# Weights loaded piece by piece between the tiles, and the levels of all tiles on VectorE, in the opening loop of a quantised cross-attention

## The chip, the cores and the metric

The kernel runs on one core of a Trainium2 chip. Five engines work side by side, each through its own list of instructions in order: PE (TensorE, matrix products; its weight loads are listed as PEld), DVE (VectorE), ACT (ScalarE), POOL (GpSimd) and SP (SyncE, which here issues the transfers between the chip's memory and the on-chip buffers). They wait for one another by semaphores. The metric is the time of one execution in microseconds on the device, lower is better.

## What is computed

Four transformer blocks follow one another over x of 4 x 1024 rows of 288, with a context of 64 rows for each of the 4. Blocks 0 and 3 have 8-bit linear layers, block 1 is a pair of cross-attentions. The change lies in block 2, whose second attention goes to the context and is fake-quantised:

```python
def _fake_quant(x, n_bits, always_zero=False):
    levels = float(2 ** n_bits - 1)
    if always_zero:
        delta = jnp.max(x) / levels
        zp = 0.0
    else:
        xmin, xmax = jnp.min(x), jnp.max(x)
        delta = (xmax - xmin) / levels
        zp = jnp.round(-xmin / delta)
    xq = jnp.clip(round(x / delta) + zp, 0.0, levels)
    return (xq - zp) * delta

def _quant_attention(x, ctx, Wq, Wk, Wv, Wo, bo):
    q, k, v = heads(x @ Wq), heads(ctx @ Wk), heads(ctx @ Wv)
    q, k, v = _fake_quant(q, 8), _fake_quant(k, 8), _fake_quant(v, 8)
    probs = softmax(q @ k.T / sqrt(18))
    probs = _fake_quant(probs, 8, always_zero=True)
    return merge(probs @ v) @ Wo + bo

h = h + _quant_attention(_ln(h), ctx, Wq2, Wk2, Wv2, Wo2, bo2)
proj = _ln(h) @ Wff1 + bff1
a, gate = jnp.split(proj, 2, axis=-1)
h = h + a * gelu(gate) @ Wff2 + bff2
```

There are 16 heads of 18. The step of the probabilities, `delta`, needs the largest probability over all rows before a single one can be rounded, so the scores are computed twice: once for their largest values and sums, once for the result.

## The kernel before

The 4096 rows are 32 tiles of 128 (`NT` = 32, 8 for each of the 4 parts of the batch). Block 2 is `fq_attn`, and its context attention and feed-forward part are `fq_tail` (L3481). Its raw queries wait in memory as `rawq`; `fq_tail` begins by loading them into `qn`, four transfers of 1152 KB, with the operands made of the keys (`kbd4`, `kbd`, `vbd`) between them.

Then comes the loop that the change touches (from L3609 on). It goes over groups `n` of four tiles. For each tile, `largest(t, qT)` (L3539) does this:

- it turns the raw queries into levels, in place: multiply by the reciprocal step and add a large constant (L819), subtract it again and take the maximum with the lower bound (L820), both in `fq_levels`; then it clips to the upper bound into one of three buffers `pads`, in bf16 (L3545). Tiles 0 to 2 and the even ones do it on DVE, the odd ones from tile 3 on POOL;
- PE transposes the four groups of heads (L3551), and ACT copies them to the group's `qT` (L3554), a buffer of which there are two, so that group `n` writes where group `n - 2` was;
- SP writes the tile's part of `qT` to memory, `qb` (L3555), for the second pass;
- PE multiplies with `kbd4` (L3558), and DVE takes the largest score of each head (L3565, `top`).

`total(n, qT)` (L3569) is a generator that runs one step after each following tile: four products (L3576) with an exponential each on ACT (L3581), their sums over the keys through products with `pick` (L3587), a copy by ACT to `sT` (L3592), products with `back` (L3596), then on DVE the sums, their reciprocals, the largest probability and its maximum (L3604 to L3607).

After the first group, the loop also loads what the feed-forward part needs: two vectors of the layer norm, the weights `w1` by `load_halves` (L2650), `w2` by `load_w` (L115), and the biases. `load_halves` loads the first 256 of the 288 rows in one transfer (L2654). The last 32 rows, which stand four times over in the array, are kept as a rounded half and a remainder: for each of six pieces of 384 columns a transfer into a scratch tile `y` with two buffers (L2660), a cast on DVE (L2661), and on the lower 64 partitions a subtraction (L2662), into the tile `w1h`. The pieces are done in one go, one behind the other. `load_halves` also serves the first attention of this block (L3031), with two pieces of 432 columns.

The order of instructions on PE, DVE, ACT and POOL is set by a scheduler from the dependences and the order of the program. On SP the order is the program's own here (`tc.manual_schedule` around `fq_tail`): an issue that waits holds up all that stand behind it.

Of the kernel before, what the change touches and what calls it, by code (L numbers as in the profile page):

```python
# [28 lines left out]
F32 = mybir.dt.float32  # L29
# [4 lines left out]
ALU = mybir.AluOpType  # L34
# [3 lines left out]
P = 128  # L38
B, S, C, H, D, T, FF = 4, 1024, 288, 16, 18, 64, 1152
# [1141 lines left out]
class Fast(Net):  # L1181
# [1465 lines left out]
            )  # L2647


    def load_halves(self, pool, scratch, w, n, name, step):  # L2650

        nc = self.nc
        t = pool.tile([P, 2, n], F32, name=name)
        nc.sync.dma_start(t, w[: 2 * P].rearrange("(c p) o -> p c o", p=P))  # L2654
        c = pool.tile([P, n], F32R, name=f"{name}h")
        for c0 in range(0, n, step):
            m = min(step, n - c0)
            cols = slice(c0, c0 + m)
            y = scratch.tile([P, step], F32, tag="w3", name="w3", bufs=2)[:, :m]
            nc.sync.dma_start(y, w[2 * P :, cols])  # L2660
            nc.vector.tensor_copy(c[:, cols], y)  # L2661
            nc.vector.tensor_tensor(  # L2662
                c[64:, cols], y[64:], c[64:, cols].bitcast(F32), ALU.subtract
            )
        return t, c

    def halves_T(self, dst, dstc, src):

# [812 lines left out]
    def fq_tail(self, w, kq, keep, rawq, mx, nmn, beside):  # L3481
# [4 lines left out]
        tc, nc = self.tc, self.nc  # L3486
        with ExitStack() as es:
            pool = lambda name, bufs, **k: es.enter_context(tc.tile_pool(name=name, bufs=bufs, **k))
# [5 lines left out]
            wp = pool("f3w", 1)  # L3494
# [7 lines left out]
            with (  # L3502
# [7 lines left out]
                qn = qp.tile([P, NT, C], F32, name="qn")  # L3510
# [8 lines left out]
                q = self.global_params(gp, mx, nmn, "qq")  # L3519
                self.watch_range(-0.5, 255.5, q["zp"], "qzext")  # L3520
                step = gp.tile([P, 1], F32, name="step")
# [17 lines left out]
                def largest(t, qT):  # L3539

                    b, j = divmod(t, NTB)
                    pd = pads[t % 3]
                    eng = nc.gpsimd if t > 2 and t % 2 else nc.vector
                    self.fq_levels(qn[:, t, :], q, 0, eng)
                    eng.tensor_scalar(  # L3545
                        pd[:, :, :D], self.heads(qn[:, t, :]), q["top"], None, ALU.min
                    )
                    ps = self.ps1(BF16)
                    pf = pd.rearrange("p h d -> p (h d)")
                    for g in range(NG):  # L3550
                        nc.tensor.transpose(  # L3551
                            ps[:, g * P : (g + 1) * P], pf[:, g * P : (g + 1) * P], self.idb
                        )
                    nc.scalar.copy(qT, ps[:, : NG * P].rearrange("p (g t) -> p g t", t=P))  # L3554
                    nc.sync.dma_start(qb[b][:, :, j * P : (j + 1) * P], qT)  # L3555
                    ps = self.ps2()
                    for g in range(NG):
                        nc.tensor.matmul(  # L3558
                            ps[:, g // 2, g % 2 * 256 : (g % 2 + 1) * 256],
                            lhsT=qT[:, g, :],  # L3560
                            rhs=kt["kbd4"][:, b, g, :],
                            start=True,
                            stop=True,
                        )
                    nc.vector.tensor_reduce(  # L3565
                        top[:, t, :], ps.rearrange("p a (h k) -> p (a h) k", k=T), AX.X, ALU.max
                    )

                def total(n, qT):  # L3569

                    es_ = []
                    for g in range(NG):
                        ps = self.ps2()
                        for pr in range(2):
                            rows = slice(pr * 64, (pr + 1) * 64)
                            nc.tensor.matmul(  # L3576
                                ps[:, pr, :], lhsT=kt["kbd"][rows, n // 2, g, :],
                                rhs=qT[rows, g, :], start=True, stop=True,
                            )
                        e = self.wk.tile([P, 2, 512], F32, tag="e1", name="e1", bufs=6)  # L3580
                        nc.scalar.activation(e, ps, AF.Exp, scale=rstep)  # L3581
                        es_.append(e)
                        yield
                    acc = self.ps1()
                    for pr in range(2):
                        for g in range(NG):
                            nc.tensor.matmul(  # L3587
                                acc[g * HP : (g + 1) * HP, :], lhsT=pick[:, pr, :],
                                rhs=es_[g][:, pr, :], start=(pr == 0), stop=(pr == 1),
                            )  # L3590
                    sT = self.wk.tile([P, 512], F32, tag="sT", name="sT", bufs=1)
                    nc.scalar.copy(sT, acc)  # L3592
                    yield
                    ps = self.ps1()
                    for j in range(4):
                        nc.tensor.matmul(  # L3596
                            ps[:, j * H : (j + 1) * H], lhsT=sT[:, j * P : (j + 1) * P],
                            rhs=back, start=True, stop=True,
                        )
                    part = lambda a: a[:, 4 * n : 4 * n + 4, :].rearrange("p t h -> p (t h)")  # L3600
                    self.ended = nc.scalar.activation(
                        part(most), part(top), AF.Exp, scale=rstep
                    ).ins
                    nc.vector.tensor_copy(part(sums), ps[:, : 4 * H])  # L3604
                    nc.vector.reciprocal(part(rs), part(sums))
                    nc.vector.tensor_tensor(part(most), part(most), part(rs), ALU.mult)
                    nc.vector.tensor_reduce(tmx[:, n : n + 1], part(most), AX.X, ALU.max)  # L3607

                running = []  # L3609
                for n in range(NT // 4):  # L3610
                    qT = self.wk.tile([P, NG, 512], BF16, tag="qT1", name="qT1", bufs=2)
                    for j in range(4):
                        largest(4 * n + j, qT[:, :, j * P : (j + 1) * P])
                        if n == 0 and j == 3:
                            nc.sync.dma_start(qT0, qb[0][:, :, : 4 * P])
                        running = [t for t in running if next(t, running) is not running]
                    running.append(total(n, qT))
                    if n == 0:
                        g3 = self.load_bc(wp, w["ln3_g"], C, "g3")
                        b3 = self.load_bc(wp, w["ln3_b"], C, "b3")  # L3620
                        nf = FF // P
                        w1 = self.load_halves(wp, qp, w["Wff13"], 2 * FF, "w1", 384)
                        w2 = self.load_w(wp, w["Wff2"], C, "w2", p=P)
                        bf1 = wp.tile([P, 2 * nf], F32, name="bf1")
                        nc.sync.dma_start(bf1, w["bff1"])
                        bf2 = self.load_bc(wp, w["bff2"], C, "bf2")
                while running:
                    running = [t for t in running if next(t, running) is not running]
                flat = lambda ap: ap.rearrange("p t h -> p (t h)")
# [170 lines left out]
            for t0 in range(0, NT, 4):  # L3800
# [14 lines left out]
                for j in range(4):  # L3815
                    next(after, None)
                    cols = slice(j * P, (j + 1) * P)
# [188 lines left out]
```

## Time and profile before

| | us |
|---|---|
| three runs: lowest, median, highest | 4733.14, 4738.31, 4739.08 |
| the profiled execution | 4733.92 |
| its span, first to last instruction | 4732.1 |
| queries loaded, first level on DVE | 2858.25 |
| first product with `kbd4` | 2865.36 |
| cast of the first piece of w1 | 2899.49 |
| copy of tile 12 by ACT | 2913.61 |
| maximum of tile 12 by DVE | 2915.33 |
| last write of `qb` issued | 2965.32 |
| end of the sums, last maximum of a probability | 2981.34 |
| products of the feed-forward part with `w1h` | 3033.7 to 3533.4 |

The profile's times of single instructions count from the start of the span. A line of the order of time reads: start, time taken, engine, line of the program, operation, tiles written and read, their shapes, how many instructions were merged into the line, and in brackets how long the engine had been idle before and what ended the idling. A line of the waits reads: who waited for whom, the sum in us, how often, and the longest. The mean TensorE clock that was granted over the whole span was 0.88 of full speed.

### The profile page before, as it was taken

The numbers are of one execution on the slowest core, as the hardware profiler recorded it, in microseconds if no ns is written. First come the engines' busy times: TensorE is split into PE (matmuls) and PEld (weight loads), VectorE is DVE, ScalarE is ACT, GpSimd is POOL, SyncE is SP. The second block draws the span as 40 slices with busy tenths as digits, with TensorE's granted clock in tenths as the row PEclk, the third lists the DMA queues.
The fourth block names the chain that finished last, engine by engine and source line by source line (L and its number), as shares of the span: only waits on it lengthen the run. The fifth ranks groups of instructions, "written<-read, shape, count | busy, mean of one in ns | idle before, by whom it ended". The sixth has DMA issues, their size and how long they took to land. (4 is left out here: it accounts for less than half of the span.)

```text
span 4732.1 us, 62855 instructions
## 1 busy us (share of the span) xinstructions
PE 4196.1 (89%) x22841; PEld 1741.1 (37%) x22841; DVE 3077.9 (65%) x6914; ACT 2999.1 (63%) x4277; POOL 1193.8 (25%) x1797
## 2 busy tenths in 40 slices
PE   4999998889988889999789986899998999998887
PEld 2223323455566531111123333455552233223444
DVE  8355445786644779999888986544346446446886
ACT  2776776566753259999799973322215776775665
POOL 2001001333210567440013343210101000002453
PEclk9999999889999875555589997899998999998898
DMA  3000002110000321000001014001001000001000
GB/s 88 2 6 22 9 11 54 56 42 6 13 13 17 113 92 42 27 18 0 14 21 29 26 29 144 21 21 19 0 19 26 2 10 26 7 12 39 15 18 19
DMA packets 138592, 135.92 MB, mean 29 GB/s; under 512 B 69404, under 2 KB 116124, under 8 KB 136736
## 3 DMA queue, kind: packets, MB, share of 16 engines
q1 hardware_dynamic: 137072, 128.13, 9.2%
q0 software_dynamic: 1200, 3.69, 0.4%
q8 instruction: 181, 2.97, 0.3%
q14 instruction: 139, 1.14, 0.1%
HBM read 79.92 MB, written 43.47 MB: 26 GB/s over the span
## 5 line engine op out<-in xcount | busy, mean ns | idle before, releaser
L2196 ACT ACTIVATE e<-ps 128x1024 f32<-128x1024 f32 x1024 | 992.6, 1021 | 412.0 <-PE ps L2186 404.6
L2186 PE MATMUL ps<-qT,kT 32*128 32x512 f32 x4096 | 624.3, 647 | 2.0 <-DVE sext L2108 2.0
L3251 DVE TENSOR_REDUCE top<-e 128x2 f32<-128x2048 f32 x256 | 563.5, 2273 | 15.4 <-ACT e L3244 15.2
L2142 PE MATMUL ps<-e,v 128*32 128x512 f32 x4096 | 553.9, 612 | 9.0 <-DVE oT L2153 9.0
L3842 PE MATMUL ps<-qk 32*128 32x512 bf16 x1024 | 500.7, 604 | 40.3 <-ACT e L3244 38.6
L3244 ACT ACTIVATE e<-ps 128x1024 f32<-128x1024 f32 x512 | 521.6, 1190 | 6.6 <-PE ps L3842 3.1
L3891 ACT ACTIVATE e<-ps 128x1024 f32<-128x1024 f32 x512 | 477.1, 1080 | 33.3 <-PE ps L3882 18.5
L3897 DVE TENSOR_SCALAR eb<-e 128x2048 bf16<-128x2048 f32 x256 | 323.8, 1270 | 48.4 <-ACT e L3891 47.3
L1921 POOL TENSOR_TENSOR x<-x,y 128x288 f32<-128x288 f32 x188 | 149.1, 805 | 812.2 <-DVE y L1919 484.8
L2693 PE MATMUL psf<-hT,w 128*128 128x512 f32 x576 | 271.9, 594 | 0.7 <-ACT hT L2684 0.6
L2186 PEld LDWEIGHTS ps<-qT,kT 32*128 32x128 f32 x4096 | 184.8, 185 | 202.1 <-issue 130.3
L3882 PE MATMUL ps<-qk,kz 64*128 64x512 bf16 x1024 | 216.7, 423 | 32.3 <-ACT e L3891 27.4
L2142 PEld LDWEIGHTS ps<-e,v 128*32 128x32 f32 x4096 | 81.3, 108 | 402.7 <-issue 345.0
L3842 PEld LDWEIGHTS <-qk 32*128 32x128 bf16 x1024 | 53.1, 99 | 465.6 <-issue 464.6
L3758 ACT ACTIVATE gl<-psf,bf 128x512 f32<-128x512 f32 x72 | 49.3, 685 | 243.6 <-PE psf L2694 235.0
L2038 POOL TENSOR_TENSOR v<-y,wv1b 128x288 f32<-128x288 f32 x64 | 51.0, 802 | 565.1 <-DVE y L2035 565.1
L3244 ACT ACTIVATION_READ_ACCUMULATOR e<-ps 128x1 f32 x512 | 192.1, 375 | 0.0
L1535 POOL TENSOR_TENSOR h<-h,g 128x288 f32<-128x288 f32 x108 | 88.0, 815 | 355.5 <-ACT h L1532 355.5
L279 PEld LDWEIGHTS <-qT 98*128 98x128 bf16 (+2 forms) x1344 | 130.1, 103 | 127.4 <-ACT qT L1437 38.9
L2153 DVE COPY oT<-ps 128x512 f32<-128x512 f32 x64 | 44.1, 689 | 202.0 <-PE ps L2142 202.0
L3762 DVE SCALAR_TENSOR_TENSOR u<-psf,bf,gl 128x512 f32<-128x512 f32 x72 | 53.6, 748 | 153.0 <-PE psf L2694 152.8
L3773 PE MATMUL psf<-w,u 128*128 128x288 f32 x576 | 147.0, 410 | 0.0
(579 smaller groups left out, 7970.4 us busy)
## 6 DMA issues: line engine op xcount, KB each, us to landing
raw<-y SPq DMA_DIRECT2D x32, 432.0 KB
in<-raw SPq DMA_DIRECT2D x30, 432.0 KB
kz<-qk SPq DMA_DIRECT2D x128, 64.0 KB
wn<-in_L_wfc SPq DMA_DIRECT2D x12, 432.0 KB
x<-in_x SPq DMA_DIRECT2D x4, 1152.0 KB
vvo<-vt SPq DMA_DIRECT2D x16, 288.0 KB
vo<-vvo SPq DMA_DIRECT2D x4, 1152.0 KB
qn<-rawq SPq DMA_DIRECT2D x4, 1152.0 KB
```

The costliest lines, as they stand in the source:

```text
L1921: eng.tensor_tensor(self.x[:, t, :], self.x[:, t, :], y, ALU.add)
L2142: nc.tensor.matmul(acc[i * HP : (i + 1) * HP, :], lhsT=st["v"][:, kt, h * (D + 1) : h * (D + 1) + HP], rhs=es_[i // 2][:, i % 2, :], start ...
L2186: nc.tensor.matmul(pss[i // 2][:, i % 2, :], lhsT=self.row_tile(kT, i)[:, kt * P : (kt + 1) * P], rhs=self.row_tile(qT, i)[:, qh * 512 : ( ...
L2196: nc.scalar.activation(e, ps, AF.Exp, scale=SCALE)
L2693: nc.tensor.matmul(o, lhsT=a[:, c, :], rhs=b[:, c, :], start=(c == 0), stop=False)
L3244: nc.scalar.activation(e[:, j, :].rearrange("p (a n) -> p a n", a=2), sc, AF.Exp, scale=rstep, accum_out=sums[:, t, h0 + j : h0 + j + 1],)
L3251: nc.vector.tensor_reduce(top[:, t, h0 : h0 + 2], e, AX.X, ALU.max)
L3773: nc.tensor.matmul(ps[:, :C], lhsT=us[f][:, j * P : (j + 1) * P], rhs=w2[:, f, :], start=(f == 0), stop=(f == nf - 1),)
L3842: self.last = self.nc.tensor.matmul(ps[:, c, :], lhsT=self.row_tile(qT, i)[:, g, qt * P : (qt + 1) * P], rhs=self.row_tile(kT, i)[:, g, c ...
L3882: nc.tensor.matmul(pss[i][:, n, :], lhsT=kz[rows, i, kt * P : (kt + 1) * P], rhs=qT[rows, g, qh * 512 : (qh + 1) * 512], start=True, stop= ...
L3891: nc.scalar.activation(e[:, 2 * n : 2 * n + 2, :], ps, AF.Exp, scale=step)
L3897: nc.vector.tensor_scalar(eb, e, MAGIC, MAGIC, ALU.add, ALU.subtract)
```

## The change

Two things are changed. `load_halves` is split: `halves_pieces` loads the first 256 rows and returns a generator that does one piece at each step. `load_halves` now runs that generator to its end and is the same as before. The loop in `fq_tail` takes the generator instead, and goes one step after each tile from tile 4 on; what is left would be done behind the loop. So the six pieces come after tiles 4 to 9, in the order of the program, and `w2` and the biases come ahead of them. Second, `largest` gives all three operations of the levels to DVE for every tile.

```diff
-    def load_halves(self, pool, scratch, w, n, name, step):
+    def halves_pieces(self, pool, scratch, w, n, name, step):
 
         nc = self.nc
         t = pool.tile([P, 2, n], F32, name=name)
         nc.sync.dma_start(t, w[: 2 * P].rearrange("(c p) o -> p c o", p=P))
         c = pool.tile([P, n], F32R, name=f"{name}h")
-        for c0 in range(0, n, step):
...
-        return t, c
+
+        def pieces():
+            for c0 in range(0, n, step):
+                m = min(step, n - c0)
+                cols = slice(c0, c0 + m)
+                y = scratch.tile([P, step], F32, tag="w3", name="w3", bufs=2)[:, :m]
+                nc.sync.dma_start(y, w[2 * P :, cols])
+                nc.vector.tensor_copy(c[:, cols], y)
+                nc.vector.tensor_tensor(
+                    c[64:, cols], y[64:], c[64:, cols].bitcast(F32), ALU.subtract
+                )
+                yield
+
+        return (t, c), pieces()
+
+    def load_halves(self, *a):
+
+        t, pieces = self.halves_pieces(*a)
+        for _ in pieces:
+            pass
+        return t
...
-                    eng = nc.gpsimd if t > 2 and t % 2 else nc.vector
-                    self.fq_levels(qn[:, t, :], q, 0, eng)
-                    eng.tensor_scalar(
+                    self.fq_levels(qn[:, t, :], q, 0)
+                    nc.vector.tensor_scalar(
                         pd[:, :, :D], self.heads(qn[:, t, :]), q["top"], None, ALU.min
                     )
...
-                running = []
+                running, pieces = [], iter(())
                 for n in range(NT // 4):
...
                         running = [t for t in running if next(t, running) is not running]
+                        next(pieces, None)
                     running.append(total(n, qT))
                     if n == 0:
...
-                        w1 = self.load_halves(wp, qp, w["Wff13"], 2 * FF, "w1", 384)
+                        w1, pieces = self.halves_pieces(wp, qp, w["Wff13"], 2 * FF, "w1", 384)
                         w2 = self.load_w(wp, w["Wff2"], C, "w2", p=P)
...
+                for _ in pieces:
+                    pass
                 while running:
```

More of the change, by code (lines that the diff above doesn't have):

```diff
@@ L2655, in load_halves @@
         c = pool.tile([P, n], F32R, name=f"{name}h")
-        for c0 in range(0, n, step):
[L2657 to L2664, printed above, removed]
-        return t, c
+        def pieces():
[15 more added lines that the diff above has]
+        return t
     def halves_T(self, dst, dstc, src):
```

## The prediction

> **What bounds the kernel now.** I read the page first, for the engines' shares, then the stage that the diff touches: its stretches, the waits of ACT and SP in it, and its instructions in order of time.
>
> ```profile
> span 4732.1 us, 62855 instructions
> PE 4196.1 (89%) x22841; PEld 1741.1 (37%) x22841; DVE 3077.9 (65%) x6914; ACT 2999.1 (63%) x4277; POOL 1193.8 (25%) x1797
> ```
>
> PE carries the kernel as a whole. The change lies in the opening loop of `fq_tail`, from 2858 to about 2981 us, where the shares differ:
>
> ```profile
> core 0: us, PE busy (x) PEld busy (x) DVE busy (x) ACT busy (x) POOL busy (x), PEclk, DMA share, GB/s
> 2876.00:2899.00 23.00, 17.11 (x92) 6.62 (x90) 18.10 (x33) 9.53 (x14) 19.22 (x21) 0.78 0.37 144
> 2899.00:2914.00 15.00, 0.09 (x2) 0.00 (x0) 5.77 (x13) 0.39 (x1) 0.00 (x0) 0.64 0.71 199
> 2930.00:2950.00 20.00, 18.14 (x120) 7.59 (x119) 12.56 (x20) 12.25 (x20) 4.00 (x4) 1.00 0.21 53
> ```
>
> In the second row 15 us pass in which PE does nothing. The waits of ACT (first line) and of SP's queue in this stage, and the instructions, tell why:
>
> ```profile
> ACT qT L3554 <- DMA qb<-qT: 15.0, 1, 15.0
> SPq L2660 <- DVE w1h L2662: 16.5, 4, 14.7
> ```
> ```profile
> 2898.07 0.58 ACT L3592 COPY sT<-ps 128x512 f32<-128x512 f32 x1 [2.10 <-PE ps L3587]
> 2899.20 0.37 DVE L3545 TENSOR_SCALAR pads<-qn,qqtop 128x288 bf16<-128x288 f32 x1 [3.79 <-PE ps L3551]
> 2899.49 0.35 DVE L2661 CAST w1h<-w 128x384 fp32r<-128x384 f32 x1
> 2905.29 0.42 SPq L115 DMA_DIRECT2D w<-in_L_Wff  x1
> 2906.45 8.97 SPq L3555 DMA_DIRECT2D qb<-qT  x10
> 2913.61 1.07 ACT L3554 COPY qT<-ps 128x512 bf16<-128x512 bf16 x2 [14.96 <-DMA qb<-qT]
> 2915.33 1.22 DVE L3565 TENSOR_REDUCE top<-ps 128x16 f32<-128x1024 f32 x1 [6.71 <-PE ps L3558]
> ```
>
> SP issues in the order of the program. It holds six loads `y`; the scratch tile has two buffers, so loads 3 to 6 wait until DVE has cast loads 1 to 4 (14.7 us for the first of them), and DVE comes to these casts at 2899.49. Behind them on SP stand the load of w2 and the writes of tiles 4 to 7 to `qb` (2906.45 on). ACT's copy of tile 12 overwrites the buffer that those writes read, so it waits until 2913.61; PE and DVE wait behind it.
>
> **The change part by part.** I write tile numbers 0 to 31, and lines as in the kernel before.
>
> *The six loads, moved between the tiles.* The number of loads, casts and subtractions is the same. On SP the order becomes: w1, w2, bf1, write 4, load 1, write 5, load 2, write 6, load 3, write 7, load 4, write 8, load 5, write 9, load 6. Load 3 still waits for the first cast and its subtraction, and write 7 stands behind load 3. So tile 12's copy still waits for the first cast, but no longer for casts 2 to 4, w2, bf1 and three writes. The question is when DVE gets to the first cast; call this time T.
>
> *The levels of 15 tiles, from POOL to DVE.* POOL loses 45 instructions, DVE gains 45: multiply-add (L819), shift and maximum (L820), clip into `pads` (L3545).
>
> ```profile
> L819 DVE TENSOR_SCALAR qn<-qn,qqrd x17: 356/597/616, 2858.3 to 2886.4; 128x288 f32<-128x288 f32 x17
> L820 DVE TENSOR_SCALAR qn<-qn,qqnzp x17: 356/556/606, 2859.1 to 2887.5; 128x288 f32<-128x288 f32 x17
> L820 POOL TENSOR_SCALAR qn<-qn,qqnzp x15: 1241/1273/1369, 2859.5 to 2892.1; 128x288 f32<-128x288 f32 x15
> L3545 POOL TENSOR_SCALAR pads<-qn,qqtop x15: 991/999/1088, 2864.1 to 2954.2; 128x288 bf16<-128x288 f32 x15
> ```
>
> DVE's shortest is 356 ns, its median 597: the long ones run while POOL runs the same operation. Starts of two pairs in the thick of it (2882.13 and 2883.16) are 1.03 apart, 0.52 an operation. Where POOL is still, a clip at 2899.20 is followed at 2899.49, one at 2930.60 at 2930.88: 0.28. POOL will be still in the changed stage, so I take 0.28 and keep 0.52 as the other end. The Trainium skill (GPSIMD Engine Reference, 1. Specifications) says that GpSimd's SBUF interface is shared with VectorE and contends with DVE's two-port modes; by it 0.28 is right everywhere once POOL is quiet. The trace agrees in part: some operations took 356 ns while POOL was busy, so no rule of it alone gives the 0.52.
>
> *T.* The instruction order of the changed program puts on DVE, from its first level (2858.25) to the first cast: 63 of the 64 level operations, 17 clips, 12 maxima (L3565) and four small ones. 80 × 0.28 = 22.4. Maxima: six took 6.88, so 1.13 apart, 12 × 1.13 = 13.6. Small ones 0.21 + 0.46 + 0.24 + 0.24 = 1.2. Sum 37.2. DVE also waits for PE. Followed through PE's order, which hardly changes, there are three waits: 0.2 before tile 6's maximum; 2.3 before tile 12's clip, whose buffer is read by tile 9's transposes, which stand behind the first `sT` copy as they did (2882.30 before, some 2 us earlier after, because the first six maxima need no clip from POOL and start near 2863.3, not 2866.41); 0.4 before tile 16's clip. With 2.9 of waits T = 2858.25 + 37.2 + 2.9 = 2898.4. That is where the first cast stood before (2899.49). So the bundle of levels that DVE takes over eats what it gains from a quiet POOL, and the stall does not go away: it only ends sooner after T.
>
> *From T to tile 12's copy.* Cast, one level in between, subtraction: 0.28 + 0.28 + 0.56 = 1.1. SP then issues load 3 (before: subtraction done at 2900.42, issue at 2900.46) and write 7 behind it, together some 0.45 on. A write lands in a quiet queue about 2.25 after its issue (the last one, 2965.32, let SP's next instruction go at 2967.6). Sum 3.9: copy at 2902.3, against 2913.61. Gain 11.3.
>
> *What is late next.* Loads 3 to 6 arrive about 2.45 after their release (2900.46 to 2902.95), so DVE casts them between the maxima of tiles 11 and 14. Casts 3 and 4 end at T + 5.5, just before tile 12's maximum can start (copy + 1.72, as 2913.61 to 2915.33). Cast 5 (0.9 with its subtraction) puts tile 13's maximum off by about 0.8, and cast 6 puts the next `sums` off by as much. PE has 1.5 us between such maxima after the stall and waits for tile 12's first; I charge 0.5. In the even run later (2930 to 2950: DVE busy 12.56 of 20) two clips more in a group of four tiles are 0.56 us per 10.6; PE's order there waits for clips nowhere, for the maxima 0.36; I charge nothing, and if that cover fails 4.5 groups × 0.56 = 2.5. POOL's clips there gain nothing either: they waited 24.2 and 6.7 us for PE and were early.
>
> w2 moved ahead of the small loads is 1.3 MB more in the queue while write 4 lands; nobody reads these until T. Load 2 and write 6 are issued long before.
>
> *PE's clock.* After the stall four L3558 matmuls take 1.03 in all (2914.26), later 0.61. The Trainium skill (TensorE: Matmul & The Clock Gate, Part 1) puts the gate to half rate after about 3.4 us of idling. The stall that is left (PE idle from about 2892 to 2903) is far above that, so by rule and row the slow start remains and the sum is unchanged; only a stall that vanished would save it.
>
> *Sum.* 11.3 − 0.5 = 10.8 us. The profiled execution took 4733.9 (span 4732.1 and 1.8 around it), 4.4 under the median of the three runs, 4738.3, and in the range that they cover (4733.1 to 4739.1). Against its own time the sum gives 4723.1; I put the forecast at the median's level: 4738.3 − 10.8 = 4727.5.
>
> **The rivals.**
>
> *Smaller gain.* The level operations need more than 0.28, say 0.33, with their semaphores (a lone chained pair, 2863.40 to 2863.79, was 0.39 apart), or the late casts hold up PE by the full 2.5. 80 × 0.05 = 4 later: gain 6.8, 4731.5. For it: chains stand in the order at a few places. Against it: nearly all are interleaved in pairs.
>
> *Slower.* DVE becomes the bound: the 0.52 is not POOL's doing but what such an operation takes in a run. Then T = 2858.25 + 80 × 0.52 + 15 = 2914.8 with the waits swallowed, tile 12's copy at 2918.7, 5.1 later than before: 4743.4, and 4744 with the 0.5. It decides from the point where T passes 2913.61 − 3.9 = 2909.7, that is at (2909.7 − 2858.25 − 15) / 80 = 0.46 per operation. For it: medians of 597 and 556. Against it: the 356 ns ones, and 0.28 wherever POOL rests.
>
> *The stall goes altogether.* DVE would cast before the remaining levels, and tile 12 would follow the `sT` copy: 15.0, and four times 0.42 of slow matmuls, 16.7: 4721.6. For it: casts need only loads that arrived by 2886. Against it: the order of the built program has some 30 levels ahead of the first cast.
>
> **How the numbers follow.** About 0.2% (9.5 us) can be told from no change here. The forecast (gain 8 to 13): 0.62; smaller gain (3 to 8): 0.22; slower: 0.08; stall gone: 0.08. Faster by over 0.2%: four fifths of 0.62 and all of 0.08, 0.58. Within: the rest of 0.62 and nine tenths of 0.22, 0.33. Slower: 0.09. The range takes in the forecast, the smaller gain and the runs' own spread of ±3: 4722 to 4736.
>
> **What would show it.** First cast (the CAST of w1h) within 2 us of 2898.4; a single wait of ACT for the write of `qb` of about 11 us; level operations at 356 ns throughout; PE's empty stretch 11 us instead of 15; the even run at 10.6 a group as before. It is wrong if the first cast comes after 2905, if level operations stay near 0.6 without POOL, or if the group time moves by over 0.3.

## The result, and the profile after

The changed kernel took 4728.66 us (median of 12 runs, 4722.06 to 4737.45), the kernel before 4738.69 us in the same comparison (12 runs, 4731.70 to 4746.81). The ratio is 0.9982, 95% interval 0.9973 to 0.9990: faster by 8.5 us, between 4.7 and 12.8; the two medians lie 10.0 apart. The forecast was 4727.5.

The profiled execution of the changed kernel took 4732.03, and its page says:

```profile
span 4730.3 us, 62834 instructions
PE 4197.2 (89%) x22841; PEld 1743.8 (37%) x22841; DVE 3083.4 (65%) x6959; ACT 2998.7 (63%) x4277; POOL 1152.0 (24%) x1752
```

That span is only 1.8 below that of the kernel before. This is no measure of the change: this execution reached the loop at 2861.68 (first level on DVE), the one of before at 2858.25. The ten profiled executions of this study came there between 2858.25 and 2867.60. From here on, times with a plus sign count from the first level of the loop in their own execution. So counted, the loop ended (end of the last maximum of a probability) at +123.31 before and at +114.09 after, 9.2 earlier, and the first product with `w1h` came at +175.52 and +165.80, 9.7 earlier. Both agree with the median. By the last instruction of the execution only 5.2 of this is left (+1873.9 and +1868.6): in these two executions, the part behind the products with `w1h`, which the change does not touch, took 4.5 longer after the change.

The busy time of each engine in three stretches, first while PE is busy ahead of tile 12, then its stall, then the even run:

```profile
2880.00:2895.40 15.40, 13.17 (x84) 5.09 (x84) 12.57 (x34) 8.47 (x12) 0.00 (x0) 1.00 0.93 327
2895.40:2907.30 11.90, 0.24 (x4) 0.07 (x2) 9.73 (x31) 0.58 (x2) 0.00 (x0) 0.57 0.20 50
2930.00:2950.00 20.00, 18.26 (x125) 8.23 (x122) 12.18 (x24) 13.24 (x20) 0.00 (x0) 1.00 0.18 46
```

Before, PE did nothing for 15 us while DVE was busy for 5.77 of them. Now PE still stands for 11.9, but DVE works through 9.73 of these: the stall is shorter. It still ends with a write to `qb`, but this write now stands behind one load that waits for DVE's first cast, no longer behind a row of loads and writes. The transfers have moved into the first stretch (DMA share 0.93). The even run looks as before.

In the changed kernel's file the lines of the loop stand 10 further on (L3554 is L3564, L3558 is L3568, L3565 is L3575), the pieces are L2662 to L2664. The waits that answer to those of before (waiter, the one it waited for, sum, times, longest):

```profile
ACT qT L3564 <- DMA qb<-qT: 11.5, 1, 11.5
DVE pads L3555 <- PE ps L3561: 3.1, 2, 1.9
SPq L2662 <- DVE w1h L2664: 10.8, 3, 9.2
```

And the order of time around tile 12:

```profile
2894.62 0.58 ACT L3602 COPY sT<-ps 128x512 f32<-128x512 f32 x1 [1.90 <-PE ps L3597]
2902.39 0.35 DVE L2663 CAST w1h<-w 128x384 fp32r<-128x384 f32 x1
2903.05 0.56 DVE L2664 TENSOR_TENSOR w1h<-w,w1h 64x384 fp32r<-64x384 f32 x1
2903.64 0.33 SPq L2662 DMA_DIRECT2D w<-in_L_Wff  x1
2904.06 0.52 SPq L3565 DMA_DIRECT2D qb<-qT  x1
2906.72 1.07 ACT L3564 COPY qT<-ps 128x512 bf16<-128x512 bf16 x2 [11.51 <-DMA qb<-qT]
2907.36 1.03 PE L3568 MATMUL ps<-kbd,qT 128*128 128x256 bf16 x4 [11.71 <-ACT qT L3564]
2908.76 1.23 DVE L3575 TENSOR_REDUCE top<-ps 128x16 f32<-128x1024 f32 x1
```

This is read from top to bottom as one chain: ACT is ready for tile 12 at 2895.2, but DVE comes to the first cast only at 2902.39; with its subtraction done, SP issues the third load, right behind it the write of tile 7, and when that write has landed ACT copies tile 12.

### The profile page after: what moved, and what is told of

Same layout as the page of the kernel before. It is cut to its first block, busy times and chain, and to the rows that moved or that the text cites. A ratio compares the mean times of both kernels' runs of the same rounds, so it can differ in the third digit from the quotient of the medians.

```text
span 4730.3 us, 62834 instructions
## 1 busy us (share of the span) xinstructions
PE 4197.2 (89%) x22841; PEld 1743.8 (37%) x22841; DVE 3083.4 (65%) x6959; ACT 2998.7 (63%) x4277; POOL 1152.0 (24%) x1752
## 3 DMA queue, kind: packets, MB, share of 16 engines
q8 instruction: 182, 2.98, 0.3%
## 4 chain that ended last, share of the span: by engine, by line
PE 54%; DVE 24%; ACT 10%; POOL 6%; issue 5%; DMA 1%; ACTq 0%; SPq 0%; DVEq 0%; POOLq 0%
PE ps L2186 10%; PE ps L2142 9%; PE psf L2704 5%; PE ps L279 5%; DVE top L3262 4%; ACT e L3904 4%; PE ps L3855 4%; PE psf L3786 3%; ACT e L3255 3%; PE ps L2910 2%; DVE eb L3910 2%; PE ps L2054 2%; PE ps L2637 1%; POOL x L1925 1%; POOL x L1921 1%
## 5 line engine op out<-in xcount | busy, mean ns | idle before, releaser
L3262 DVE TENSOR_REDUCE top<-e 128x2 f32<-128x2048 f32 x256 | 563.5, 2278 | 16.8 <-ACT e L3255 16.7
```

Of the source, the lines that this page charges most:

```text
L3262: nc.vector.tensor_reduce(top[:, t, h0 : h0 + 2], e, AX.X, ALU.max)
```

## Experiments

All eight were timed against the kernel before: 4737.76 for the first four, 4738.55 for the last four. Each has 5 to 11 runs (e5 and e6 only 5). The intervals of many ratios overlap, those of the changed kernel, e1, e2, e3 and e8 almost wholly: the medians don't put these five in an order. The first cast, tile 12's copy, its maximum, and the loop's end come from each kernel's one profile. In e8 the first level itself comes 6 us late, as told there.

| kernel | median, us | ratio, 95% interval | first cast | copy | maximum | loop's end |
|---|---|---|---|---|---|---|
| before | | | +41.23 | +55.36 | +57.08 | +123.31 |
| changed | 4728.66 | 0.9982, 0.9973 to 0.9990 | +40.70 | +45.03 | +47.07 | +114.09 |
| e1 pieces alone | 4726.21 | 0.9980, 0.9971 to 0.9989 | +41.23 | +45.26 | +47.24 | +113.30 |
| e2 levels alone | 4730.08 | 0.9983, 0.9974 to 0.9992 | +35.40 | +51.02 | +52.74 | +118.70 |
| e3 casts on POOL | 4726.18 | 0.9976, 0.9967 to 0.9985 | +32.89 | +37.56 | +46.74 | +111.13 |
| e4 pieces late | 4720.81 | 0.9969, 0.9957 to 0.9981 | +43.36 | +33.70 | +41.10 | +109.17 |
| e5 late, POOL | 4719.77 | 0.9958, 0.9944 to 0.9971 | +44.31 | +40.36 | +41.65 | +105.86 |
| e6 late, held | 4713.91 | 0.9955, 0.9942 to 0.9969 | +38.04 | +33.79 | +35.08 | +104.95 |
| e7 pieces, held | 4724.53 | 0.9971, 0.9959 to 0.9982 | +34.34 | +38.36 | +40.48 | +106.13 |
| e8 loads on POOL's queue | 4728.38 | 0.9980, 0.9971 to 0.9990 | ahead of the loop | +38.51 | +47.37 | +112.11 |

### e1 and e2: one half of the change at a time

e1 is the changed kernel with the levels given back:

```diff
-                    self.fq_levels(qn[:, t, :], q, 0)
-                    nc.vector.tensor_scalar(
+                    eng = nc.gpsimd if t > 2 and t % 2 else nc.vector
+                    self.fq_levels(qn[:, t, :], q, 0, eng)
+                    eng.tensor_scalar(
```

> The pieces go between the tiles, odd tiles' levels stay on POOL. Times from the first level of the loop: copy of tile 12 stood at 55.4 us before and at 45.0 after the change. My theory (the copy waits for the first cast and the few issues behind it): the order has the first cast where it was, at 41.2, so the copy comes at about 45.3, the loop's end some 9.5 us earlier than before, the time about 4729. Rival (the gain came from levels that a quiet POOL no longer slows): no gain beyond 2 us from this part, about 4737.

e2 is the kernel before with the same three lines turned the other way.

> All levels on DVE, the six pieces in one go as before. In this kernel's order only 44 levels stand ahead of the first cast (63 in the changed one), so the first cast comes at about 35.5 us from the first level. By my theory loads 3 to 6, w2 and four writes still stand in SP's queue: casts 3 and 4 near 39, load 6 issued near 41, tile 12's copy 8.7 after that as before, at 49.5; gain about 5.5 us, time about 4733. Rival (parts add up, and the pieces are all of the gain): the copy stays near 55, the time within 2 us of before. Rival (a quiet POOL is the whole gain): copy at 45, time 4728.

In e1 the first level groups of DVE, and one line of the order of time (the cast came at 2900.33, the copy at 2904.36):

```profile
L819 DVE TENSOR_SCALAR qn<-qn,qqrd 128x288 f32<-128x288 f32 x17 | 8.3, 523 | 0.8 <-DMA qn<-rawq 0.8
2904.36 1.07 ACT L3565 COPY qT<-ps 128x512 bf16<-128x512 bf16 x2 [4.86 <-DMA qb<-qT]
```

Half as many level operations on DVE, each slower by POOL's work (523 ns in the mean against 365 in the changed kernel): the first cast stands at +41.23, within 0.6 of the changed kernel, and the loop ends 0.8 earlier than there. ACT's wait is only 4.86, because tile 11's copy comes at +34.2 here and at +27.2 in the changed kernel; tile 12's comes at the same time in both. So up to the loop's end the pieces bring the whole gain of the change, and the move of the levels adds nothing that these runs show. (By the first product with `w1h` this order is turned round: +167.90 in e1, +165.80 in the changed kernel. From the loop's end to that product the ten profiles took between 51.7 and 54.6, so differences under some 3 us there tell nothing.)

In e2, in the order of time:

```profile
2899.52 0.36 DVE L2661 CAST w1h<-w 128x384 fp32r<-128x384 f32 x1
2900.77 5.78 SPq L2660 DMA_DIRECT2D w<-in_L_Wff  x4
2906.60 0.43 SPq L115 DMA_DIRECT2D w<-in_L_Wff  x1
2907.76 9.20 SPq L3554 DMA_DIRECT2D qb<-qT  x10
2915.15 1.07 ACT L3553 COPY qT<-ps 128x512 bf16<-128x512 bf16 x2 [17.50 <-DMA qb<-qT]
```

The scheduler places the casts otherwise here, and the first comes 5.8 earlier than before. But four loads, w2 and then the writes still follow one another on SP, and the copy comes 15.6 behind the cast (14.1 before, 4.3 in the changed kernel). The copy gains 4.3, 1.5 less than expected, and the loop 4.6. Alone, then, the levels do bring a part of what the pieces bring; the two shorten the same stall, by 4.6 and 10.0 alone and by 9.2 together at the loop's end, and don't add up. This rests on one profile each; the medians can't tell e2 from the changed kernel.

### e7: the cast sets the copy

The changed kernel, but DVE does the levels of tile t (from tile 10 on) only behind the maximum of tile t-5, so that 34 instead of 63 level operations stand ahead of the first cast:

```diff
-                    self.fq_levels(qn[:, t, :], q, 0)
+                    with tc.issue_after(tops[t - 5]) if t >= 10 else nullcontext():
+                        self.fq_levels(qn[:, t, :], q, 0)
```

> The changed kernel (pieces from the second group on) with the levels of tile t (from tile 10 on) queued on DVE behind the maximum of tile t-5: 34 instead of 63 level operations stand ahead of the first cast. Theory of the prediction (tile 12's copy follows the first cast by some 4.3, and the cast comes when DVE has done what stands ahead of it): the first cast at 33 to 34.5 instead of 40.7 (29 x 0.28 = 8.1 earlier, or when its load has landed, if that is later), tile 12's copy at 37 to 39 instead of 45.0, its maximum 1.8 later, the loop's end at 106 to 108 instead of 114.1, the time 6 to 8 us below the changed kernel's. Rival (the stall in the changed kernel is w2 and the small loads in the queue, not the cast): the copy stays at 43 to 45 though the cast is early.

```profile
2900.87 0.35 DVE L2663 CAST w1h<-w 128x384 fp32r<-128x384 f32 x1
2904.89 1.07 ACT L3565 COPY qT<-ps 128x512 bf16<-128x512 bf16 x2 [4.77 <-DMA qb<-qT]
```

The cast came 6.4 earlier than in the changed kernel and the copy 6.7 earlier, 4.0 behind the cast as there. The rival, in which transfers hold the copy, falls. The loop ended 8.0 earlier. The median is 4.1 below the changed kernel's, short of the expected 6 to 8, and the intervals of the two ratios overlap, so the gain in time over the changed kernel is not shown by the medians; the first product with `w1h` came 7.4 earlier.

### e4 and e8: the write freed from the loads

e4 starts the pieces only in the fourth group, so that the writes of tiles 4 to 11 stand ahead of all of them:

```diff
-                        next(pieces, None)
+                        if n > 2:
+                            next(pieces, None)
```

> The changed kernel, but the pieces start only after tile 12, when DVE has all levels behind it; casts stay on DVE. My theory: writes 4 to 7 stand behind nothing, ACT does not wait for them, tile 12's maximum comes when DVE's bundle of 24 levels ends, at about 41 us from the first level; the casts then fall into a stretch where DVE is busy 63%: 6 us less than the changed kernel, time about 4722. Rival (the stall moves to the next waiting load: a write behind loads 3 to 6 holds up a later copy): copy of tile 12 early but a new wait of ACT for a write of qb of 5 us or more, time 4728.

```profile
2895.93 1.07 ACT L3564 COPY qT<-ps 128x512 bf16<-128x512 bf16 x2 [0.19 <-DMA qb<-qT]
2896.50 0.65 DVE L820 TENSOR_SCALAR qn<-qn,qqnzp 128x288 f32<-128x288 f32 x2
2897.06 0.65 DVE L819 TENSOR_SCALAR qn<-qn,qqrd 128x288 f32<-128x288 f32 x2
...
2903.33 2.35 DVE L3575 TENSOR_REDUCE top<-ps 128x16 f32<-128x1024 f32 x2
2904.60 0.61 PE L3586 MATMUL ps<-qT,kbd 64*128 64x512 bf16 x2 [5.75 <-DVE top L3575]
2906.80 1.03 PE L3568 MATMUL ps<-kbd,qT 128*128 128x256 bf16 x4
```

ACT's wait of 11.5 is 0.2 here: the stall at the copy came from the order on SP. A new wait takes a part of its place. The scheduler has put the levels of the last tiles in one bundle on DVE; 24 of these operations stand ahead of tile 12's maximum, which comes 7.4 behind the copy, and PE waits 5.75 for it. The loop ends 4.9 earlier than in the changed kernel.

e8 leaves the pieces where the changed kernel has them and issues their loads from POOL's queue, which is empty:

```diff
-                nc.sync.dma_start(y, w[2 * P :, cols])
+                q.dma_start(y, w[2 * P :, cols])
...
-                        w1, pieces = self.halves_pieces(wp, qp, w["Wff13"], 2 * FF, "w1", 384)
+                        w1, pieces = self.halves_pieces(wp, qp, w["Wff13"], 2 * FF, "w1", 384, nc.gpsimd)
```

> The changed kernel with the six small loads issued by POOL's queue instead of SP's; casts and subtractions on DVE and the same count of everything. Theory (the stall comes from the order on SP's queue alone: a write of qb stands behind a load that waits for a cast): tile 12's copy at 33.7 to 34.5 as in e4, ACT's wait for the write of qb under 1, the loop's end at 108 to 112, the time 3 to 7 us below the changed kernel's. Rival (the small loads slow the writes of qb in the DMA engines, whichever queue issues them): the copy at 40 or later with an ACT wait for qb above 5. A third way: the casts now come early in DVE's order and DVE waits for their loads ahead of the levels; then the whole loop is late from its start.

ACT has no wait for the write of `qb` among its waits in this stage, so the theory of the queue holds; but the time is as in the changed kernel. The waits and the order of time say where it went:

```profile
PEld L3562 <- DVE pads L3556: 17.1, 5, 10.3
POOL w L2663 <- DVE w1h L2665: 15.3, 3, 12.0
```
```profile
2861.83 0.36 DVE L2664 CAST w1h<-w 128x384 fp32r<-128x384 f32 x1 [4.85 <-DMA w<-in_L_Wff]
2865.45 1.03 PE L3562 MATMUL ps<-idb,pads 128*128 128x128 bf16 x8 [10.18 <-DVE pads L3556]
2912.54 0.61 PE L3587 MATMUL ps<-qT,kbd 64*128 64x512 bf16 x2 [7.20 <-DVE top L3576]
```

The casts now stand early in DVE's order, two of them ahead of the loop, the others among its first levels. DVE waits 4.85 for the first load before it starts the loop, which is the third way of the expectation: the first level comes 11.5 behind the clearing of `pads` on POOL, in the other nine profiles 5.4 to 5.6. PE's wait of 10.3 is the one for the first clip of the loop, 4.2 in the changed kernel. These 6 us lie ahead of the point from which the plus times count, so e8's are too good by 6 beside the others. In the loop itself tile 12's copy is at +38.5, later than expected, and the bundle of levels stands behind it as in e4 (maximum at +47.4); PE waits 7.2 for that maximum. One queue was unblocked and another engine's list lengthened.

### e3: the casts on POOL

The changed kernel with the casts and subtractions of w1 on POOL, which has nothing else to do in this loop:

```diff
-                nc.vector.tensor_copy(c[:, cols], y)
-                nc.vector.tensor_tensor(
+                eng.tensor_copy(c[:, cols], y)
+                eng.tensor_tensor(
```

> The changed kernel with casts and subtractions of the six pieces on POOL, which is idle there. No issue of SP waits for DVE any more. My theory: ACT's wait of 11.5 us for the write of qb is gone; the next that is late is DVE, which has 24 levels ahead of tile 12's maximum, so this maximum comes at about 41 us from the first level (47.1 in the changed kernel, 57.1 before): 6 us less than the changed kernel, time about 4722. If POOL's casts slow DVE's levels to 0.52 us apart while they run, up to 4 us of that is lost, 4726. Rival (the casts were not what held the copy, the transfers were): copy stays near 45, time 4728.

```profile
2900.49 0.50 POOL L2664 CAST w1h<-w 128x384 fp32r<-128x384 f32 x1 [36.23 <-DMA w<-in_L_Wff]
2902.16 1.72 DVE L820 TENSOR_SCALAR qn<-qn,qqnzp 128x288 f32<-128x288 f32 x2
2903.80 0.64 DVE L819 TENSOR_SCALAR qn<-qn,qqrd 128x288 f32<-128x288 f32 x2
2904.36 0.64 DVE L820 TENSOR_SCALAR qn<-qn,qqnzp 128x288 f32<-128x288 f32 x2
2905.16 1.07 ACT L3565 COPY qT<-ps 128x512 bf16<-128x512 bf16 x2 [4.23 <-DMA qb<-qT]
2914.34 2.35 DVE L3576 TENSOR_REDUCE top<-ps 128x16 f32<-128x1024 f32 x2
```

POOL casts as soon as the load has landed, and the copy comes 4.7 behind the cast, at +37.56. ACT's wait for the write, expected to be gone, is 4.23, since load 3 still waits, now for POOL's first cast. But tile 12's maximum comes at +46.74, hardly earlier than in the changed kernel. It stands behind the bundle of levels, and a pair of these takes 1.64 while POOL casts and subtracts (2902.16 to 2903.80) and 0.56 while it rests (2903.80 to 2904.36). The expectation had the mechanism and too small a price for it: the maximum is 5.6 behind that of e4.

### e5 and e6: the bundle of levels

e5 is e4 with the odd tiles' levels back on POOL; e6 is e4 with the levels of tile t queued behind the maximum of tile t-6.

> As e4 (pieces only from the fourth group of tiles on), but the levels of the odd tiles stay on POOL as in the kernel before. Times from the first level of the loop. Theory (the two places for the levels cost the same, since DVE's own operations are slowed by POOL's): DVE has 34 instead of 64 level operations ahead of tile 12's maximum, but at 0.52 instead of 0.28 each, 17.7 instead of 17.9; tile 12's copy stays at 33.7, its maximum at 41 +- 2, the loop's end at 109 +- 2, the time within 3 us of e4's. Rival (the levels on DVE pay once no stall covers them): tile 12's maximum after 44, the time 4 us or more above e4's. Second rival (with fewer levels in the way the maximum comes right behind the copy): maximum at 35.5 to 38, the time 4 us below e4's.

> As e4, but the levels of tile t (from tile 10 on) are queued on DVE behind the maximum of tile t-6, so that the 24 levels that stood ahead of tile 12's maximum in e4 are spread over the later groups. Theory (in e4 that bundle is what tile 12 waits for after its copy): tile 12's copy at 33.7 as in e4, its maximum at 35.4 to 37 instead of 41.1, the loop's end at 104 to 105.5 instead of 109.2, the time about 4.5 us below e4's. Rival (the same levels now stand in the way of the clips and maxima of the even run, 24 x 0.28 = 6.7): maximum early, but the groups take 11.5 or more instead of 10.6 and the loop's end stays at 108 to 110, the time as e4's.

e5's maximum came at +41.65, as its theory has it, and its time lies 1.0 under e4's; the copy however came at +40.36, not at +33.7, and the loop ended at +105.86, under the expected 109 ± 2. The copies were late already ahead of tile 12 (tile 11's at +34.35, at +27.20 in e4): PE waited 3.36 for the maximum of tile 8, which stood behind DVE's levels and came at +29.82 (+24.48 in e4). So with the levels on DVE the copy came 6.7 earlier (e4), and the bundle on DVE took that back ahead of the maximum. e5's loop ends 3.3 before e4's, which lost time later: the last two casts, three maxima and four clips follow one another on DVE there, PE waits 2.59 for one of these clips, and tile 21's copy is 6.2 behind tile 20's (4.3 in e5).

In e6:

```profile
2893.10 1.07 ACT L3565 COPY qT<-ps 128x512 bf16<-128x512 bf16 x2
2894.39 1.23 DVE L3576 TENSOR_REDUCE top<-ps 128x16 f32<-128x1024 f32 x1 [0.49 <-PE ps L3569]
```

The maximum follows the copy in 1.3, at +35.08, and DVE waits for PE there, not PE for DVE. The loop ends at +104.95 and the time is 4713.91, the lowest of this study: ratio 0.9955 (0.9942 to 0.9969), an interval that overlaps those of e4 and e5. The rival fell: from tile 21 on a group takes 10.5. Only here do the levels on DVE pay (maximum 6.6 before e5's), but the loop's end keeps just 0.9 of it, and the first product with `w1h` nothing (+158.47, +158.34 in e5): the copies of tiles 18 and 19 lie 5.9 apart and those of 20 and 21 6.5, where the even run has 1.7 and 4.3. The order of time shows the cause:

```profile
2914.32 0.40 PE L3562 MATMUL ps<-idb,pads 128*128 128x128 bf16 x4 [3.26 <-DVE pads L3556]
2915.40 1.03 PE L3569 MATMUL ps<-kbd,qT 128*128 128x256 bf16 x4 [0.68 <-ACT qT L3565]
```

The last casts (+49.89 and +53.33) fall between tiles 18 and 19; the clip behind them is late, and PE waits 3.26 for it. After that pause PE is slow again (1.03 for four products), at a granted clock of 0.50 from 2916 to 2921, and tile 21 falls into this stretch. Spreading the casts further was not tried.

## Why the prediction was right, point by point

- *The cause of the stall* (a write of `qb` behind a load, behind a cast): right, shown by e4 and e8, where the write is freed and ACT's wait goes, and by e7, where the copy moves with the cast.
- *T*, from the first level to the first cast: 40.15 predicted, 40.70 measured (2902.39 against the 2898.4 of the prediction; 3.4 of these 4.0 are the later start of the loop). By the starts in the trace, 80 level operations and clips took 22.7 (22.4 predicted), 12 maxima 13.6 (13.6), the small ones 1.0 (1.2), the waits 3.4 (2.9). The wait at tile 12's clip was 1.9 (2.3), at tile 16's 1.2 (0.4), at tile 6's maximum 0.3 (0.2).
- *The price of 0.28 a level operation where POOL rests*: right; the 32 of L819 in the changed kernel lie at 365 ns in the mean, and pairs follow every 0.56. With it the rival "slower" fell, and "smaller gain" by 0.33 an operation. *That DVE's bundle eats what it gains from a quiet POOL*: right, T was +41.23 before and is +40.70; e1 shows no gain from the move of the levels.
- *From T to the copy*: 3.9 predicted (its terms, 1.1, 0.45 and 2.25, add up to 3.8), 4.33 measured. Cast to the issue of load 3 took 1.25 (1.1), the write landed 2.66 behind its issue (2.25, taken from a write with no load ahead of it in the queue).
- *Gain at the copy*: 11.3 predicted, 10.33 measured (55.36 less 45.03), the two terms above.
- *The late casts*: 0.5 charged, 1.3 measured. From tile 12's copy to tile 17's took 17.82 in the changed kernel and 16.50 before: 0.4 up to tile 16, 0.9 behind it. The first part is the casts' and was charged about right: tile 13's maximum came 2.24 behind tile 12's, 1.50 before (0.7 against 0.8).
- *PE's clock after the stall*: right that the slow start remains (four products took 1.03 from 2907.36 until tile 16's, and 0.61 from 2921.43), wrong that it leaves the sum unchanged. This is the term that was mis-sized most, nothing charged for 0.9. In the changed kernel PE started again at 2907.36, and the granted clock was 0.50 until 2920 and 1.00 from 2921; before, it started at 2914.26 and had 0.50 until 2923 and 1.00 from 2924. So the slow stretch is some 4 us longer, and tile 17 falls into it: ten products with `pick` took 3.19 from 2918.30, where ten of them took 1.90 at a clock of 1.00 (2892.63), and DVE waited 2.98 for PE meanwhile. How far the casts, by the pauses they gave PE, made the stretch longer is not shown.
- *The even run*: charged at nothing, and right. The copies of tiles 17, 21, 25 and 29 lie 10.59, 10.58 and 10.58 apart, before 10.63, 10.62 and 10.62.
- *Sum*: 10.8 predicted; 9.2 at the loop's end, 9.7 at the first use of `w1h`, 8.5 by the ratio and 10.0 between the medians. The misses at the copy (1.0) and behind it (0.8) point the same way, so neither hid the other. The gain by the ratio, 0.18%, lies at the lower end of the forecast's 8 to 13 us and just under the 0.2% that the prediction thought more likely to be passed than not.
- *The stall gone altogether*: no such thing in the changed kernel, as its order on DVE said. It needed the pieces behind tile 12 (e4) and the levels spread (e6), and then gave 18.4 at the loop's end, near the 16.7 of that rival, with one pause of PE left (3.26 in e6).

## What to carry to other kernels

A transfer that waits for a buffer on an in-order queue delays everything behind it there, so look up which later write or load some other engine will need, and move the waiting ones behind that, not only apart. When the wait is gone, look at what the engine on the other end does in the meantime: here a scheduler had packed 24 operations, each for a later tile, ahead of the one that was due, and spreading them brought the loop's end another 4.2 forward (e4 to e6), after the 4.9 of moving the loads (the changed kernel to e4). Two measures that shorten the same stall are to be priced together, never added.

## What was not expected of the hardware

- DVE's level operations followed each other at 0.28 with POOL at rest, at 0.52 with the same operations on POOL, and at 0.82 while POOL cast and subtracted two inputs (pairs of 1.64 in e3). Work on POOL is not free for DVE, and its price depends on what POOL does.
- PE stayed slow long after its stall. In the changed kernel it started again at 2907.36, was busy for 4.42 of the 5 us from 2910 and 3.98 of those from 2915, and the granted clock was 0.50 in both; only from 2920 to 2925 was it 0.91. In e4 it started again at 2904.60 and had 1.00 from 2911. The Trainium skill (TensorE: Matmul & The Clock Gate, Part 1) gives some 3.4 us of sustained work until the gate opens; PE's work here had short pauses in it, and the gate opened after 6 us in e4 and over 12 in the changed kernel. That a pause well under the old stall is enough to close the gate, as the same part of the Trainium skill has it, e4 shows: after 5.75 us the four products took 1.03. Shorter ones were enough too: in e6 one of 3.26, and in e4 one of 2.59, up to 2924.32 (1.04 for the four products from 2926.59). Both lie under the 3.4 us of idling that the prediction quotes from there, so that figure is no safe bound here.
- The same program ahead of the loop took from 2858.25 to 2867.60 us in nine profiled executions of nine kernels (all but e8). That spread is as large as the gain, so a single profile's span can't judge such a change; a stage counted from its own first instruction can, unless the change delays that instruction itself, as e8 does.
